# A gated delta-net layer with a table-coded FFN: substitution steps moved within the slots, FFN weight pieces gathered in one slot

## The chip, the cores and the metric

The kernel runs on one core of a Trainium2 chip. The metric is the device time of one execution in microseconds (us). Three executions of the kernel before took 4345.69, 4349.83 and 4350.42 us; the median is 4349.83 us.

## The reference

The input is `x` of 4 x 1024 x 256 in f32. Two residual blocks are applied, each with a layer norm before and after it. The first is a gated delta net with 16 key heads and 32 value heads of 128, worked in chunks of 64 tokens:

```
mixed = silu(conv4(x @ W_qkv))             # causal convolution over 4 tokens
q, k = l2n(q), l2n(k)
A  = -(k_beta @ k.T * decay) * strict      # per chunk and head, 64 x 64
Tm = solve_triangular(eye - A, eye)        # unit lower triangular inverse
u, kcd = Tm @ v_beta, Tm @ (k_beta * exp(gc))
# scan over the chunks, with a state St of 128 x 128 per head
v_new = u - kcd @ St
out   = (q * exp(g)) @ St + (q @ k.T * decay) @ v_new
St    = St * exp(g_last) + (k * exp(g_last - g)).T @ v_new
y = (rmsnorm(out) * norm_w * silu(x @ W_z)) @ W_out
```

The second block is an FFN, `silu(gate) * up`, whose three weight matrices are given as indices into a table of 16 values (`w = lut[idx]`).

## The kernel before, in words

The work is cut into 8 groups of 4 value heads. In a group there are 32 units: one chunk of 64 tokens of two batch rows together, so that 128 rows are filled. 8 units make a "super"; there are 32 supers. The compute engines' order is written out by hand: each engine runs its instructions in exactly the order in which the program issues them, and so does SyncE's DMA queue, and each instruction waits by semaphore for what it needs.

The main loop (line 1024 on) goes over **slots**, one for each unit of the scan, with a lead of 21 slots for preparation. A slot is written as a string of names in `SLOTS`, picked by `iq`, the slot's place in its super, so the pattern repeats every 8 slots; "slot 5" below is the slot with iq 5. What the names issue:

- `A` and `B`: one `channel` each, a projection of 128 channels (`pp`, 8 matmuls, L423) and its convolution: one tap on ScalarE (`cv`, L437), then three on VectorE (L440) that are put off by a place or two, then silu on ScalarE (L444).
- `N0`, `N1`, `N2`: the newer unit's `step`: transposes of v (`pv`) and their scaling to `x0`; the state's products (`pkqs`, L684) with four VectorE operations that add them to `x0` (L695) and `qs` on ScalarE; then the inverse times `x0` (`px`, L704), `yg` from it on VectorE (L712), and the state's decay on GpSimd (`S`, L721).
- `O3`, `J`, `O4`: the older unit's end: `po` and `core` (L728), the sums of squares on ScalarE (`junk`, L733), then `pu` (L741) and the state's update on VectorE (`S`, L748).
- `Z`, `T`, `U`: the gated output: `pz` (L143) and silu `zs` (L782) at `Z`; two GpSimd products `zs` (L784, L786), issued one and two places behind it; `pto` and `oT`; `pout` (L797) and the sum `ac` on VectorE (L802).
- `n`, `s`, `r`, `q`: norms, scores and rms. Scores end in `kkq` with `lT` and `aT` on VectorE (L556) in slots 2, 3, 6 and 7; in between, GpSimd forms the decay matrix `dc`: four operations (L530, L531) issued at the end of slots 0 and 4, and two (L537) at the end of slots 1 and 5, after exponentials on ScalarE (L534).
- `v1`: one call of `invert`, the **forward substitution**: 32 matrices of 32 x 32 in each of four partition groups are inverted column by column. The first call loads `lb` and sets `v`; each of the 31 others is one step j with two VectorE operations, an outer product `rank` (L580) and its subtraction from `v` (L581), both of (j+1)(31-j) elements per partition (31 to 256), and both with two operands in SBUF. A number behind the `v` is the number of calls.
- `b`: `build`, in slots 3 and 4. It begins with a ScalarE copy of `v` (`lb`, L593) and sends `v` through DRAM into the padded matrices of the matmuls `m` (L612, L626).

A super's inversion begins in slot 4 and is spread over slots 4 to 7, 0, 1 and 2; what is left of it at the end of slot 2 is drained there (`if inv and iq == 2`). After `O4` each slot also issues one **piece** of the FFN's weights (`next(pieces, None)`): one GpSimd comparison with a table entry (L301, TENSOR_SCALAR) and one addition (L305, TENSOR_TENSOR). There are 224 pieces.

PSUM gives the main loop four single banks and two double ones (`two_banks`). The double ones are used in turn by A's `pp`, `pu` and B's `pp`, so a slot's `pu` writes the bank that the preceding slot's B filled, and must wait for that B's last `cv` tap.

Of the kernel before, what the change touches and what calls it, by code (L numbers as in the profile page):

```python
# [15 lines left out]
B, S, HID = 4, 1024, 256  # L16
# [48 lines left out]
def delta_net_ffn_kernel(  # L65
# [18 lines left out]
    V, A, G_, T_ = nc.vector, nc.scalar, nc.gpsimd, nc.tensor  # L84
# [84 lines left out]
    def layer_norm_stats(pool, src, n, tag):  # L169

        mv = pool.tile([P, n, 2], F32, tag=f"mv{tag}", name=f"mv{tag}")
        for i in range(n):
            st = pool.tile([P, 6], F32, tag=f"st{tag}", name=f"st{tag}")
            V.bn_stats(st, src(i))
            V.bn_aggr(mv[:, i, :], st)
        r = pool.tile([P, n], F32, tag=f"r{tag}", name=f"r{tag}")
        G_.tensor_scalar_add(r, mv[:, :, 1], LN_EPS)
        G_.tensor_tensor(r, r, bc(rsqrt, [P, n]), ALU.pow)
        return mv, r
# [14 lines left out]
    with tc.tile_pool(name="pre", bufs=2) as pre, tc.tile_pool(name="gates", bufs=1) as gp:  # L194
# [13 lines left out]
        for s in range(NSB):  # L208
# [4 lines left out]
            mv, r = layer_norm_stats(pre, lambda i: xt[:, i, :], SB, "a")  # L213
# [70 lines left out]
    def lut_pieces(pool):  # L284

        jobs = []
        for n, idx in ((0, gidx), (1, uidx)):
            for r in range(KC):
                for h in range(INTER // PIECE):
                    rows, cols = slice(r * P, (r + 1) * P), slice(h * PIECE, (h + 1) * PIECE)  # L290
                    jobs.append((idx[rows, cols], wgu_d[n, rows, cols], P, PIECE))
        for r, n in I_TILES:
            jobs.append((didx[r : r + n, :], wd_d[r : r + n, :], n, HID))
        for src, dst, n, cols in jobs:
            ix = pool.tile([P, PIECE], I32, tag="lx", name="lx")
            w = pool.tile([P, PIECE], F32, tag="lw", name="lw")
            nc.sync.dma_start(ix[:n, :cols], src)
            for e in range(NLUT):
                t = pool.tile([P, PIECE], F32, tag="lt", name="lt") if e else None
                o = t if e else w  # L300
                G_.tensor_scalar(  # L301
                    o[:n, :cols], ix[:n, :cols], float(e), lutb[:n, e : e + 1], ALU.is_equal, ALU.mult
                )
                if e:
                    G_.tensor_add(w[:n, :cols], w[:n, :cols], t[:n, :cols])  # L305
                yield
            nc.sync.dma_start(dst, w[:n, :cols])

    with ExitStack() as main:
# [4 lines left out]
        pieces = lut_pieces(sc)  # L314
# [500 lines left out]
        def resume(gen):  # L815
            nonlocal count
            wait = next(gen, None)
            if wait:
                heappush(due, (place + wait, count, gen))
                count += 1  # L820

        def go(gen):

            nonlocal place
            late = [entry for entry in due if entry[2] is gen]
            while late:
                due.remove(late[0])
                heapify(due)
                resume(gen)
                late = [entry for entry in due if entry[2] is gen]  # L830
            if gen is not None:
                resume(gen)
            place += 1
            while due and due[0][0] <= place:
                resume(heappop(due)[2])
# [7 lines left out]
        def work(kind, n, *args):  # L843

            if not 0 <= n < len(supers):
                return None
            key = (kind, n, *args)
            if key not in started:
                started[key] = kind(supers[n], *args)
            return started[key]  # L850
# [3 lines left out]

        LQ = 2 * SB + 5
        LV = SB // 2
        SLOTS = [
            "A v1 O3 s N0 v1 T n J O4 v1 N1 Z v1 B n N2 U n s",  # L860
            "A v1 O3 N0 v1 T J v1 O4 N1 r Z v1 B N2 q s U",
            "A v1 O3 N0 v1 T J v1 O4 v1 N1 Z s v1 B N2 n U",
            "b A O3 N0 T J O4 N1 Z s B N2 U b",
            "v1 A b O3 s N0 v1 T n J O4 v1 N1 Z v1 B n N2 v1 U n s",
            "A v1 O3 N0 v1 T J v1 O4 v1 N1 r Z v1 B N2 q s v1 U",
            "A v1 O3 N0 v1 T J v1 O4 v1 N1 Z s v1 B N2 n v1 U",
            "A v1 O3 N0 v1 T J v1 O4 v1 N1 Z s v1 B N2 v1 U",
        ]


# [152 lines left out]
        with tc.manual_schedule(engines=COMPUTE):  # L1023
            for s in range(-LQ, len(units)):
                n, i = divmod(s, SB)
                nq, iq = divmod(s + LQ, SB)
                nv, iv = divmod(s + LV, SB)
                gens = {}
                newer = step(*units[s]) if s >= 0 else None
                for c in "01234":  # L1030
                    gens["N" + c], gens["O" + c] = newer, older
                gens["J"] = older
                gens["T"] = gens["U"] = gated
                gated = project_out(*units[s - OUT_LAG]) if s >= OUT_LAG else None
                gens["Z"] = gated
                if 0 <= nv < len(supers):
                    gens["A"] = channel(supers[nv], iv // 4, 2 * MG + iv % 4, 2)
                if nq < len(supers):
                    gens["B"] = channel(supers[nq], iq // 4, iq % 4, 1)
                inv = work(invert, nq - 1 if iq >= 4 else nq - 2)  # L1040
                made = work(build, nq - 2)

                root = [work(rms, *divmod(s // 4 - 1, 2))] + ([work(roots, n + 1)] if i == 4 else [])

                ahead = units[s + 1] if 0 <= s + 1 < len(units) else None
                if ahead and ahead[1]:
                    expand(*ahead)
                for name in SLOTS[iq].split():
                    c = name[0]
                    if c == "v":  # L1050
                        for _ in range(int(name[1:]) if inv else 0):
                            next(inv, None)
                        continue
                    block = 2 * nq + iq // 4 - (iq % 4 != 2 or c == "s")
                    if c in "rq":
                        for gen in filter(None, root[: 1 if c == "r" else 2]):
                            resume(gen)
                        continue
                    if c == "n":
                        gen = work(norms, *divmod(block, 2))  # L1060
                    elif c == "s":
                        gen = work(scores, *divmod(block, 2))
                    elif c == "b":
                        gen = made
                    else:
                        gen = gens.get(name)
                    go(gen)
                    if name == "O4":
                        next(pieces, None)
                        if ahead and not ahead[1]:  # L1070
                            expand(*ahead)
                if inv and iq == 2:
                    drain(inv)
                older = newer
                if s >= EARLY:
                    next(early, None)
            drain(older)
            drain(rms(supers[-1], 1))
            drain(*(gen for _, _, gen in sorted(due)))
            drain(early)  # L1080
            last_ffn()
            rest = [gated] + [project_out(*unit) for unit in units[len(units) - OUT_LAG :]]
            part = gate_up(0)
            while rest or part:
                for gen in rest[:2]:
                    if next(gen, END) is END:
                        rest.remove(gen)
                if part and next(part, END) is END:
                    part = None
            for v in range(NU):  # L1090
                nxt = gate_up(v + 1) if v + 1 < NU else None

                side = [ended(v - 1, range(4))] if v else []
                if 4 <= v + 2 < NU:
                    side.append(prepared(v + 2))
                    next(side[-1])
                side = chain(*side)
                if nxt:
                    next(nxt)
                for i in range(4):  # L1100
                    down(v, i)
                    next(side, None)
                    if not nxt:
                        drain(ended(v, [i]))
                while nxt and next(nxt, END) is not END:
                    next(side, None)
                drain(side)
# [51 lines left out]
```

## Time and profile before

| | |
|---|---|
| median of 3 runs | 4349.83 us |
| the profiled execution: its own time, its span | 4347.06 us, 4345.3 us |
| granted TensorE clock, mean | 0.98 |
| busy: TensorE, VectorE, ScalarE, GpSimd | 92%, 81%, 61%, 48% of the span |
| `rank` (L580) and `v` (L581), 992 operations each | 467.2 and 553.3 us on VectorE |
| pieces (L301 and L305), all forms | some 470 us on GpSimd, the last one at 3269.7 us |
| first and last `rank` | 172.4 and 3906.3 us |

Reading: PE is TensorE's matmuls, DVE is VectorE, ACT ScalarE, POOL GpSimd, SP SyncE. A row of a group gives the line, the engine, the operation, what it writes and reads, the shape and the count; behind the bar are the busy time, the mean of one in ns, and the engine's idle time just before. A row of the timeline gives start, duration, engine, line, operation and, in brackets, how long the engine sat idle before and for whom. A row of windows gives a stretch, its length, and for each engine its busy time and number of instructions in it.

The main loop's steady part is a chain of 32 supers of about 121 us each. The slots of one of them begin with A's `pp` at 1781.7 (slot 4), 1797.6 (5), 1813.6 (6), 1830.3 (7), 1845.8 (0), 1860.4 (1), 1873.4 (2) and 1888.0 us (3); the next super begins at 1902.9 us.

### The profile page before, as it was taken

The numbers are of one execution on the slowest core, as the hardware profiler recorded it, in microseconds if no ns is written. First come the engines' busy times: TensorE is split into PE (matmuls) and PEld (weight loads), VectorE is DVE, ScalarE is ACT, GpSimd is POOL, SyncE is SP. The second block draws the span as 40 slices with busy tenths as digits, with TensorE's granted clock in tenths as the row PEclk, the third lists the DMA queues.
The fourth block names the chain that finished last, engine by engine and source line by source line (L and its number), as shares of the span: only waits on it lengthen the run. The fifth ranks groups of instructions, "written<-read, shape, count | busy, mean of one in ns | idle before, by whom it ended". The sixth has DMA issues, their size and how long they took to land.

```text
span 4345.3 us, 79442 instructions
## 1 busy us (share of the span) xinstructions
PE 3992.3 (92%) x26664; PEld 2858.5 (66%) x26664; DVE 3517.0 (81%) x6641; ACT 2646.9 (61%) x6573; POOL 2082.5 (48%) x1782
## 2 busy tenths in 40 slices
PE   3679999999999999999999999999999999999999
PEld 3456667677666666676766667676766776666454
DVE  4788888888888888888888988888888898886243
ACT  2456667666666666666666666666666666656211
POOL 2545564655555554655455554555554343434122
PEclk7899999999999999999999999999999999999999
DMA  3444444444444454444454444544445444443011
GB/s 88 124 107 113 111 112 124 121 130 119 126 130 118 107 133 125 134 117 119 125 135 128 109 114 128 133 118 114 132 128 128 115 120 121 130 108 96 26 39 29
DMA packets 1053124, 492.72 MB, mean 113 GB/s; under 512 B 730528, under 2 KB 951856, under 8 KB 1052720
## 3 DMA queue, kind: packets, MB, share of 16 engines
q1 hardware_dynamic: 1052720, 487.64, 42.5%
q8 instruction: 216, 3.54, 0.3%
q14 instruction: 188, 1.54, 0.1%
HBM read 267.66 MB, written 219.69 MB: 112 GB/s over the span
## 4 chain that ended last, share of the span: by engine, by line
PE 57%; DVE 25%; issue 7%; ACT 6%; POOL 3%; DMA 1%; SPq 1%; DVEq 0%; POOLq 0%; ACTq 0%
PE pp L423 13%; DVE cv L440 9%; PE pout L797 7%; PE pz L143 7%; PE pkqs L684 6%; DVE rank L580 4%; PE pgu L960 4%; PE px L704 4%; PE pu L741 3%; PE po L704 3%; DVE v L581 2%; PE kkq L546 2%; PE py L976 2%; DVE core L728 2%; PE pto L790 1%
## 5 line engine op out<-in xcount | busy, mean ns | idle before, releaser
L440 DVE SCALAR_TENSOR_TENSOR cv<-pp,cw,cv 128x512 f32<-128x512 f32 x1536 | 1148.9, 748 | 352.2 <-ACT cv L437 322.7
L784 POOL TENSOR_TENSOR zs<-zs,rr 128x512 f32<-128x512 f32 x256 | 267.0, 1043 | 1558.3 <-ACT zs L782 1549.3
L437 ACT ACTIVATE cv<-pp,cw 128x512 f32<-128x512 f32 x512 | 350.9, 685 | 486.0 <-PE pp L423 486.0
L581 DVE TENSOR_TENSOR v<-v,rank 128x31 f32<-128x31 f32 (+15 forms) x992 | 553.3, 558 | 34.1
L423 PE MATMUL pp<-xnT,wq 128*128 128x262 f32 x2048 | 531.0, 401 | 43.3 <-DVE cv L440 34.6
L423 PEld LDWEIGHTS pp<-xnT,wq 128*128 128x128 f32 x2048 | 371.7, 191 | 216.6 <-issue 58.7
L423 PE MATMUL pp<-xnT,wv 128*128 128x262 f32 x2048 | 503.0, 387 | 5.8 <-DVE cv L440 5.8
L797 PE MATMUL pout<-wo,oT 128*128 128x256 f32 x2048 | 504.9, 391 | 0.7 <-ACT oT L792 0.7
L143 PE MATMUL pz<-wzs,xnT 128*64 128x512 f32 x2048 | 487.1, 596 | 4.7 <-DVE ac L802 3.8
L580 DVE TENSOR_TENSOR rank<-v,lb 128x31 f32<-128x31 f32 (+15 forms) x992 | 467.2, 471 | 25.9 <-DMA lb<-ltd 20.1
L684 PE MATMUL pkqs<-S,qku 128*64 128x256 f32 x3840 | 478.1, 387 | 5.2 <-DVE core L728 3.5
L721 POOL TENSOR_TENSOR S<-S,dkm 128x1024 f32<-128x1024 f32 x224 | 436.7, 1949 | 26.5 <-PE pkqs L684 16.1
L704 PE MATMUL px<-x,ue 128*128 128x128 f32 x2048 | 292.9, 287 | 168.2 <-issue 108.1
L704 PEld LDWEIGHTS px<-x,ue 128*128 128x128 f32 x2048 | 264.1, 194 | 269.0 <-issue 151.1
L423 PEld LDWEIGHTS pp<-xnT,wv 128*128 128x128 f32 x2048 | 381.5, 190 | 73.8 <-issue 13.1
L797 PEld LDWEIGHTS pout<-wo,oT 128*128 128x128 f32 x2048 | 384.1, 198 | 49.4 <-issue 3.4
L684 PEld LDWEIGHTS pkqs<-S,qku 128*64 128x64 f32 x3840 | 248.7, 136 | 204.2 <-issue 49.2
L733 ACT ACTIVATE junk<-core 128x128 f32<-128x128 f32 x1024 | 318.5, 311 | 82.4 <-DVE core L728 53.9
L786 POOL TENSOR_TENSOR zs<-zs,core 128x512 f32<-128x512 f32 x256 | 328.6, 1284 | 20.0
L709 ACT ACTIVATE xs<-px 128x512 f32<-128x512 f32 x256 | 154.8, 605 | 236.2 <-PE px L704 236.2
L444 ACT ACTIVATE qk<-cv 128x512 f32<-128x512 f32 x256 | 161.2, 630 | 206.1 <-DVE cv L440 202.6
L741 PE MATMUL pu<-yg,kt 64*128 64x256 f32 x1920 | 272.2, 402 | 14.5 <-DVE cv L440 13.1
(187 smaller groups left out, 7198.4 us busy)
## 6 DMA issues: line engine op xcount, KB each, us to landing
qkd<-qk SPq DMA_DIRECT2D x256, 256.0 KB, 2.6
qku<-qkd SPq DMA_DIRECT2D x256, 256.0 KB, 2.9
dc<-rows_d SPq DMA_DIRECT2D x256, 128.0 KB, 3.4
ltd<-lT SPq DMA_DIRECT2D x128, 256.0 KB, 2.5
atd<-aT SPq DMA_DIRECT2D x128, 256.0 KB, 2.8
ae<-atd SPq DMA_DIRECT2D x512, 64.0 KB, 2.6
acc_d<-ac SPq DMA_DIRECT2D x256, 128.0 KB, 2.2
ac<-acc_d SPq DMA_DIRECT2D x224, 128.0 KB, 2.6
```

The lines of the kernel that those rows point to most:

```text
L143: T_.matmul(ps[ab * C : (ab + 1) * C, :], lhsT=xnT[:, kc, 2 * p + ab, H + n * C : H + (n + 1) * C], rhs=rhs(kc), start=kc == 0, stop=kc == ...
L423: T_.matmul(ps[:, 2 * p : 2 * p + 2, : H + BT], lhsT=wt[:, kc, :], rhs=xnT[:, kc, 2 * p : 2 * p + 2, c0 : c0 + H + BT], start=kc == 0, sto ...
L437: A.activation(cv, ps[:, :, H : H + BT], AF.Copy, scale=cw[:, ch, H : H + 1])
L440: V.scalar_tensor_tensor(cv, ps[:, :, i : i + BT], cw[:, ch, i : i + 1], cv, ALU.mult, ALU.add)
L580: V.tensor_tensor(t, bc(v[:, 0 : j + 1, j : j + 1], sh), bc(lb[:, j : j + 1, j + 1 :], sh), ALU.mult)
L581: V.tensor_tensor(v[:, 0 : j + 1, j + 1 :], v[:, 0 : j + 1, j + 1 :], t, ALU.subtract)
L684: T_.matmul(as4(ps)[ab * C : (ab + 1) * C, two, :], lhsT=qk[:, m, j, ab, :], rhs=S_[:, ab, two, :], start=True, stop=True,)
L704: T_.matmul(as4(ps)[:, h, :], lhsT=w[:, h, :], rhs=src[:, h, :], start=True, stop=True)
L721: G_.tensor_tensor(flat, flat, bc(decay, [P, 2 * HG, P]), ALU.mult)
L741: T_.matmul(as4(pu[:, ab])[:, two, :], lhsT=kt[half, m, :], rhs=yg[half, two, :], start=True, stop=True)
L786: G_.tensor_tensor(zs, zs, k.cores.pop(u), ALU.mult)
L797: T_.matmul(pp[:, :HID], lhsT=oT[:, h, :], rhs=wo[:, h, :], start=h == 0, stop=h == HG - 1)
```

## The change

The calls of `invert` are put at other places of the slot strings, and their number per slot changes; the pieces are issued by a table, 0, 1 or 3 to a slot.

```diff
+        PIECES = 1, 0, 1, 3, 1, 0, 1, 0
         SLOTS = [
-            "A v1 O3 s N0 v1 T n J O4 v1 N1 Z v1 B n N2 U n s",
-            "A v1 O3 N0 v1 T J v1 O4 N1 r Z v1 B N2 q s U",
-            "A v1 O3 N0 v1 T J v1 O4 v1 N1 Z s v1 B N2 n U",
+            "A v1 O3 s v1 N0 v1 T n J O4 N1 v2 Z B n N2 U n s",
+            "A O3 N0 T J O4 N1 v2 r Z B N2 q s U",
+            "A v1 O3 v1 N0 v2 T J O4 N1 v2 Z s B N2 n U",
             "b A O3 N0 T J O4 N1 Z s B N2 U b",
-            "v1 A b O3 s N0 v1 T n J O4 v1 N1 Z v1 B n N2 v1 U n s",
-            "A v1 O3 N0 v1 T J v1 O4 v1 N1 r Z v1 B N2 q s v1 U",
-            "A v1 O3 N0 v1 T J v1 O4 v1 N1 Z s v1 B N2 n v1 U",
-            "A v1 O3 N0 v1 T J v1 O4 v1 N1 Z s v1 B N2 v1 U",
+            "v1 A b O3 s v1 N0 v1 T n J O4 N1 v2 Z B n N2 U n s",
+            "A O3 N0 T J O4 N1 v2 r Z B N2 q s U",
+            "A v1 O3 v1 N0 v1 T J O4 N1 v2 Z s B N2 n U",
+            "A v1 O3 v1 N0 v2 T J O4 N1 v2 Z s B N2 U",
         ]
...
                     if name == "O4":
-                        next(pieces, None)
+                        for _ in range(PIECES[iq]):
+                            next(pieces, None)
```

The steps j that fall into each slot, in the order in which a super's inversion runs:

| slot | 4 | 5 | 6 | 7 | 0 | 1 | 2 | 3 |
|---|---|---|---|---|---|---|---|---|
| before | load, 0-3 | 4-9 | 10-15 | 16-21 | 22-25 | 26-29 | 30 | none |
| changed | load, 0-3 | 4-5 | 6-10 | 11-16 | 17-21 | 22-23 | 24-29, and 30 at the slot's end | none |
| pieces, changed | 1 | 0 | 1 | 0 | 1 | 0 | 1 | 3 |

No step stands behind `Z` or between `T` and `N1` any more; in slots 4, 6, 7, 0 and 2 steps stand in the first part of the slot too, and in each slot with steps two stand between `N1` and `Z`.

## The prediction

> **What bounds the kernel now.** I read the page first (chain, groups), then the windows of the eight slots of one super, then the timeline of the worst slot, engine by engine.
>
> ```profile
> PE 57%; DVE 25%; issue 7%; ACT 6%; POOL 3%; DMA 1%; SPq 1%; DVEq 0%; POOLq 0%; ACTq 0%
> ```
>
> TensorE holds most of the chain, VectorE a quarter. The windows tell in which slots (length, then busy time and count of PE, PEld, DVE, ACT, POOL):
>
> ```profile
> 1781.70:1797.60 15.90, 15.90 (x130) 11.04 (x127) 9.85 (x21) 11.17 (x28) 7.98 (x8) 1.00 0.52 120
> 1797.60:1813.60 16.00, 13.37 (x84) 9.68 (x83) 15.44 (x30) 8.14 (x22) 11.31 (x10) 1.00 0.41 94
> 1813.60:1830.30 16.70, 14.38 (x100) 10.55 (x100) 16.32 (x29) 12.79 (x30) 10.71 (x9) 1.00 0.28 67
> 1830.30:1845.80 15.50, 14.07 (x99) 10.60 (x98) 15.15 (x29) 7.87 (x23) 6.40 (x5) 1.00 0.60 179
> 1845.80:1860.40 14.60, 14.60 (x95) 10.18 (x94) 12.86 (x28) 9.03 (x25) 2.73 (x3) 1.00 0.45 125
> 1860.40:1873.40 13.00, 13.00 (x84) 9.80 (x83) 12.58 (x24) 8.88 (x23) 11.66 (x10) 1.00 0.29 75
> 1873.40:1888.00 14.60, 14.37 (x100) 10.57 (x100) 13.43 (x25) 13.13 (x32) 7.60 (x8) 1.00 0.48 131
> 1888.00:1902.90 14.90, 14.90 (x131) 11.29 (x129) 10.58 (x19) 9.66 (x24) 8.05 (x9) 1.00 0.71 196
> ```
>
> These are slots 4, 5, 6, 7, 0, 1, 2, 3. In 4, 0, 1 and 3 PE is never idle. In 5, 6 and 7, with six steps each, it idles 2.63, 2.32 and 1.43 us and VectorE hardly at all: there VectorE bounds. The timeline of slot 6 shows why (the last two rows are GpSimd's and PE's):
>
> ```profile
> 1823.54 1.23 DVE L748 TENSOR_TENSOR S<-pu,S 128x1024 f32<-128x1024 f32 x1
> 1824.68 0.82 DVE L580 TENSOR_TENSOR rank<-v,lb 128x252 f32<-128x252 f32 x1
> 1825.54 1.37 DVE L581 TENSOR_TENSOR v<-v,rank 128x252 f32<-128x252 f32 x1
> 1826.83 1.11 DVE L695 SCALAR_TENSOR_TENSOR x<-pkqs,dkm,x 128x128 f32<-128x128 f32 x4
> ...
> 1825.31 1.32 POOL L786 TENSOR_TENSOR zs<-zs,core 128x512 f32<-128x512 f32 x1
> ...
> 1827.37 1.13 PE L704 MATMUL px<-x,ue 128*128 128x128 f32 x8 [2.07 <-issue]
> ```
>
> One step stands ahead of `x`; its `rank` ends 0.27 us behind the `zs` product L784 (1824.19 to 1825.23), its `v` 0.28 us behind L786 (1826.63). PE waits 2.07 us. The same operations alone take little more than one ns an element; by size:
>
> ```profile
> L581 DVE TENSOR_TENSOR v<-v,rank 128x135 f32<-128x135 f32 x64 | 68.5, 1070 | 2.2
> L581 DVE TENSOR_TENSOR v<-v,rank 128x156 f32<-128x156 f32 x64 | 20.8, 325 | 2.2
> ```
>
> Fewer elements take three times as long: the place in the slot decides, not the size. 156 elements at 325 ns and 256 at 425 give 0.17 us + 1.0 ns an element; the 31 steps have 5456 elements, so 2 x (31 x 0.17 + 5456 x 0.001) = 21.5 us a super, against (467.2 + 553.3)/32 = 31.9 measured. So **10.4 us a super are waits on GpSimd's TENSOR_TENSORs**, one for one.
>
> **What the change does, part by part.** A super costs 120.4 us ((3906.3 - 172.4)/31, from the `rank` rows). I scale by 30, for 32 supers of which some at group ends are shorter.
>
> *Pieces.* In the super from 3343.4 us no piece runs any more (GpSimd's L301 busy 0.00), and it takes 121.6 us, against 121.2 with eight pieces. So moving them is worth 0, at most 0.4 x 30 = 12 us either way. Three in slot 3 (2.4 us each by the rows, 1.44 + 0.92) delay nobody there: the next GpSimd work, `zs` at 1897.4, comes 9.4 us behind the slot's start. No wait, load or queue is added: each piece's DMAs move with it past at most three slots, and the last piece is done about slot 257 of 277 instead of 225, 4 slots ahead of `begin_ffn`.
>
> The Trainium skill, "SBUF — State Buffer", § Who interferes with whom, says that a VectorE instruction with two SBUF inputs contends with any GpSimd instruction that reads SBUF, and that the second to issue blocks fully. The rows agree for TENSOR_TENSOR, but not for the pieces' TENSOR_SCALAR: during L301 (1828.76, 1.44 us) `v` on 255 elements took 0.42 us. By the page each L301 met by a step would cost up to 1.44 us; for the three slots freed of theirs that would make the sum 3 x 1.44 x 30 = 130 us lower.
>
> *Slot 5, two steps instead of six.* Both come behind `x`. Slot 1 has the same tiles and takes 13.0 us with PE always busy: 16.0 to about 13.2, **-2.7** (no more, since the mean super is 0.8 us shorter than this one).
>
> *Slot 6, five instead of six, three of them ahead of `x`.* Slot 2 has the same tiles, so I start from its rows: ScalarE, behind the exponentials, ends its `cv` at 6.29 us into the slot and VectorE's first tap starts at 6.33. Behind it now come tap 0.75, step 7 0.8 (+0.5 behind the piece's L305), two taps 1.55, step 8 0.85, `S` 1.2, `x` 1.1: done at 13.1; PE starts `px` about 0.55 us ahead of that (as at 1827.37, with `x` ending 1827.94), and 2.9 us later the slot ends (1827.37 to 1830.3): 15.4 instead of 16.7. **-1.2.**
>
> *Then the two steps between `N1` and `Z`: the new place is not ahead of the `zs` products.* L784 starts 2.56 us behind the last tap (1882.09 to 1884.65 in slot 2: silu of `vt`, four `qs`, silu of `zs` on ScalarE). VectorE needs `S` + `x` = 2.3 us plus its steps from there. In slots 6, 7 and 2, with steps behind the taps, the pair thus starts when `zs` does. In slot 6: taps done at 10.0, L784 12.5 to 13.55, L786 to 14.85, `S` decay (1.95) to 16.85. From 13.1 the four operations wait for one each: 13.8, 15.1, 17.1, 17.5; alone they would end at 14.8. Queued behind them are `lT`, `aT`, B's taps, `yg`: 1.3 + 0.75 + 0.7 + 1.5 = 4.25, until 21.7, **6.3 us into slot 7** (now 2.46). `pu` needs that bank and starts 3.6 us into an unhindered slot: 2.7 late.
>
> *Slot 7.* From 6.3: `ac` 0.35, step 0.9, `core` 0.65, tap 0.75, step 0.9, two taps 1.55, two steps 1.85, `S` 1.2, `x` 1.1 = 15.55; minus 0.55 plus 2.9 = 17.9, against 15.5 here; I take **+1.5**, since slot 7 varies with slot 6. Its pair waits for L786 and the decay (to about 18.2), ends at 19.35, the tail at 23.6, 5.7 into slot 0.
>
> *Slot 0.* `pu` 2.1 late; now PE is never idle there: **+1.6**. Norms keep `zs` later in this slot, so its pair is free and VectorE catches up. *Slot 1:* pair, `eq` and `rr` against the same three GpSimd products, as `eq` and `rr` alone today: 0.
>
> *Slot 2, seven steps instead of one.* Four ahead of `x` add 2.6 less today's wait of 1.4 (step 30): `px` 0.7 to 2.6 late, **+1.2**. *Slot 3:* the second pair collides as in slot 6, the tail reaches 5.7 into slot 3, `pu` 2.1 late; and step 30, now last in slot 2, ends near 6.4, so `lb` on ScalarE (2.0 us) starts there, not at 1.59, with A's `cv` queued behind it: **+2.2**, nothing less than 0.2. SP holds `vd` for step 30 with later loads behind it, used a slot later. Slot 3's four idle microseconds (14.9 - 10.58 on DVE) of VectorE then absorb the rest.
>
> **Sum:** -2.7 - 1.2 + 1.5 + 1.6 + 0 + 1.2 + 2.2 = **+2.6 us a super**, x 30 = +78. The profiled execution has 4347; 4425, and 3 more for the median: **4428 us**.
>
> **Rivals.** *Faster: the waits go.* If ScalarE's silu comes later than I have it, or VectorE gets ahead, the pair slips in before `zs` in every slot. Then slot 5 gives -2.7, 6 and 7 -2.0 and -1.0, and slot 3 costs 0.3 to 1.5: -5.4 to -4.2 a super, 4188 to 4224. For it: slot 4's and slot 3's gaps behind `x` (0.6 us and more). Against: the 2.56 us above hold `zs` and `x` together. In between, with slots 7 and 0 at half of my price and slots 2 and 3 at +1.5, the super is -0.9, 4323. Chance of faster, both: 0.28.
>
> *Level:* gains of slots 5 and 6 just pay for the rest: 4341 to 4359, 0.06.
>
> *Slower, and worse:* slots 7 and 0 at full price (+2.4, +2.1) and slot 2 at +2.6: +5.4 a super, 4510. Of the 0.66 for slower, my sum has 0.45 and this 0.21.
>
> **The numbers.** Likeliest's own range 4370 to 4490. For 8 in 10 I leave out the better half of the faster case (0.12) and the end of the worse (0.07): 4240 to 4500. About 0.2% can be told from no change in this measurement: faster 0.28, within 0.06, slower 0.66.
>
> **What would show it.** Right: PE idle gone in slot 5, about as long idle in 7, new in 0, 2 and 3, ahead of `pu` by `cv` L440; mean of `v` and `rank` hardly below 558 and 471 ns; `lb` L593 waiting for `v`. Wrong: `v` and `rank` near 350 ns, and PE never idle in slots 6 and 7; then the pair stands ahead of `zs`, and my coupling of `zs` to the last tap is the step that fails.

## The result, and the profile after

The changed kernel takes **4444.01 us** (median of 4 runs, 4442.11 to 4445.07) against 4347.76 of the kernel before on the same chip: a ratio of 1.0222, 95% interval 1.0204 to 1.0239. The forecast was 4428, range 4240 to 4500. The profiled execution's span is 4442.0 us, 96.7 more than before.

The page's chain has moved from TensorE to VectorE, ScalarE and DMA:

```profile
PE 47%; DVE 31%; ACT 9%; DMA 5%; issue 5%; SPq 2%; POOL 1%; DVEq 0%; ACTq 0%; POOLq 0%
```

The windows of the changed kernel, for one super from slot 4 to slot 3 (columns as in the prediction):

```profile
1839.50:1855.50 16.00, 16.00 (x131) 11.10 (x128) 9.92 (x22) 11.16 (x28) 10.90 (x11) 1.00 0.66 159
1855.50:1868.50 13.00, 13.00 (x85) 9.77 (x84) 10.93 (x24) 8.17 (x22) 8.42 (x8) 1.00 0.47 114
1868.50:1882.80 14.30, 14.10 (x100) 10.52 (x99) 11.51 (x21) 12.77 (x30) 7.85 (x8) 1.00 0.46 111
1882.80:1900.60 17.80, 15.80 (x100) 11.44 (x99) 17.45 (x29) 7.87 (x23) 6.12 (x5) 0.90 0.39 117
1900.60:1916.80 16.20, 14.88 (x95) 10.16 (x94) 15.78 (x30) 9.01 (x25) 3.54 (x3) 1.00 0.50 133
1916.80:1929.80 13.00, 13.00 (x84) 9.79 (x83) 12.58 (x23) 8.74 (x23) 10.27 (x9) 1.00 0.30 78
1929.80:1945.20 15.40, 14.34 (x99) 10.53 (x99) 14.99 (x27) 13.18 (x32) 8.42 (x8) 1.00 0.27 71
1945.20:1963.50 18.30, 15.62 (x132) 11.27 (x130) 15.36 (x27) 9.68 (x24) 12.52 (x11) 1.00 0.63 165
```

Slot 5 (second row) no longer idles on PE and takes 13.0 us instead of 16.0, slot 6 14.3 instead of 16.7. Slots 7, 0, 2 and 3 are longer, and there PE now idles 2.0, 1.3, 1.1 and 2.7 us while VectorE is busy nearly throughout in slots 7, 0 and 2. Mean slot lengths, over 24 supers of each trace (from one start of A's `pp` to the next):

| slot | 4 | 5 | 6 | 7 | 0 | 1 | 2 | 3 | super |
|---|---|---|---|---|---|---|---|---|---|
| before | 15.62 | 15.13 | 16.00 | 16.32 | 14.62 | 13.00 | 14.38 | 14.92 | 120.0 |
| changed | 16.01 | 12.32 | 14.14 | 16.47 | 17.03 | 13.00 | 15.18 | 18.85 | 123.0 |
| forecast difference | 0 | -2.7 | -1.2 | +1.5 | +1.6 | 0 | +1.2 | +2.2 | +2.6 |
| measured difference | +0.4 | -2.8 | -1.9 | +0.2 | +2.4 | 0 | +0.8 | +3.9 | +3.0 |

3.0 us on 32 supers are the 96.7. Two things lie behind these means. Slot 7 takes 15.5 us before in three supers of four, and 17.6 to 19.7 in every fourth; in the changed kernel it takes mostly 16.8, and 14.6 to 14.7 in every fourth. And in slot 7 of the super shown the granted clock is at 0.50 for 3.4 us (0.90 over the slot): the five slots 7 of the changed kernel with such a stretch take 17.8 to 18.0 us.

The pair between `N1` and `Z` of slot 6, in the timeline of the changed kernel, VectorE first, then GpSimd:

```profile
1879.32 1.11 DVE L695 SCALAR_TENSOR_TENSOR x<-pkqs,dkm,x 128x128 f32<-128x128 f32 x4
1880.36 0.77 DVE L580 TENSOR_TENSOR rank<-v,lb 128x220 f32<-128x220 f32 x1
1881.16 1.34 DVE L581 TENSOR_TENSOR v<-v,rank 128x220 f32<-128x220 f32 x1
1882.53 1.98 DVE L580 TENSOR_TENSOR rank<-v,lb 128x231 f32<-128x231 f32 x1
1884.54 0.40 DVE L581 TENSOR_TENSOR v<-v,rank 128x231 f32<-128x231 f32 x1
...
1879.84 1.04 POOL L784 TENSOR_TENSOR zs<-zs,rr 128x512 f32<-128x512 f32 x1 [3.92 <-ACT zs L782]
1880.95 1.30 POOL L786 TENSOR_TENSOR zs<-zs,core 128x512 f32<-128x512 f32 x1
1882.21 2.04 POOL L721 TENSOR_TENSOR S<-S,dkm 128x1024 f32<-128x1024 f32 x1
```

Each of the first three ends 0.25 us behind one GpSimd product: 1881.13 behind 1880.88, 1882.50 behind 1882.25, 1884.51 behind 1884.25; the fourth, free, takes 0.40. What stands behind them is late for TensorE in slot 7:

```profile
1886.20 0.66 PE L671 MATMUL pv<-ident,vt 128*128 128x128 f32 x4 [0.59 <-DVE aT L556]
1887.54 0.63 PE L790 MATMUL pto<-ident,zs 128*128 128x128 f32 x4 [0.69 <-DVE yg L712]
1888.89 2.08 PE L741 MATMUL pu<-yg,kt 64*128 64x256 f32 x8 [0.72 <-DVE cv L440]
```

`pu` starts 6.1 us into the slot; the prediction had 6.3. `pv` and `pto` wait too, for PSUM banks that `aT` and `yg` still read. Over the whole run, PE's idle time ahead of `pu` (behind the second bar; before, then changed):

```profile
L741 PE MATMUL pu<-yg,kt 64*128 64x256 f32 x1920 | 272.2, 402 | 14.5 <-DVE cv L440 13.1
L741 PE MATMUL pu<-yg,kt 64*128 64x256 f32 x1920 | 279.7, 411 | 64.5 <-DVE cv L440 64.5
```

Ahead of `pz` it grows from 4.7 to 33.4 us, 33.0 of them for `x0` from ScalarE.

### The profile page after: what moved, and what is told of

The parts are those of the page before. It is cut to its first block, busy times and chain, and to the rows that moved or that the text cites. A ratio compares the mean times of both kernels' runs of the same rounds, so it can differ in the third digit from the quotient of the medians.

```text
span 4442.0 us, 79504 instructions
## 1 busy us (share of the span) xinstructions
PE 4022.4 (91%) x26664; PEld 2854.2 (64%) x26664; DVE 3602.9 (81%) x6641; ACT 2643.1 (60%) x6573; POOL 2078.5 (47%) x1782
## 4 chain that ended last, share of the span: by engine, by line
PE 47%; DVE 31%; ACT 9%; DMA 5%; issue 5%; SPq 2%; POOL 1%; DVEq 0%; ACTq 0%; POOLq 0%
PE pp L423 10%; DVE cv L440 8%; DVE rank L580 6%; PE pz L143 6%; PE pkqs L684 5%; DVE v L581 5%; PE pout L797 4%; PE pgu L962 4%; PE px L704 3%; PE pu L741 3%; PE po L704 2%; DVE S L748 2%; DVE x L695 2%; PE py L978 2%; PE pn L474 1%
## 5 line engine op out<-in xcount | busy, mean ns | idle before, releaser
L580 DVE TENSOR_TENSOR rank<-v,lb 128x31 f32<-128x31 f32 (+15 forms) x992 | 508.5, 513 | 60.8 <-DMA lb<-ltd 45.2
L143 PE MATMUL pz<-wzs,xnT 128*64 128x512 f32 x2048 | 487.2, 596 | 33.4 <-ACT x L675 33.0
L797 PE MATMUL pout<-wo,oT 128*128 128x256 f32 x2048 | 486.6, 381 | 0.7 <-ACT oT L792 0.7
L423 PEld LDWEIGHTS pp<-xnT,wv 128*128 128x128 f32 x2048 | 384.6, 192 | 76.4 <-issue 14.1
L797 PEld LDWEIGHTS pout<-wo,oT 128*128 128x128 f32 x2048 | 370.7, 191 | 44.6 <-issue 3.4
L143 PEld LDWEIGHTS pz<-wzs,xnT 128*64 128x64 f32 x2048 | 141.3, 137 | 230.4 <-issue 150.0
```

The source lines that it names most:

```text
L143: T_.matmul(ps[ab * C : (ab + 1) * C, :], lhsT=xnT[:, kc, 2 * p + ab, H + n * C : H + (n + 1) * C], rhs=rhs(kc), start=kc == 0, stop=kc == ...
L423: T_.matmul(ps[:, 2 * p : 2 * p + 2, : H + BT], lhsT=wt[:, kc, :], rhs=xnT[:, kc, 2 * p : 2 * p + 2, c0 : c0 + H + BT], start=kc == 0, sto ...
L580: V.tensor_tensor(t, bc(v[:, 0 : j + 1, j : j + 1], sh), bc(lb[:, j : j + 1, j + 1 :], sh), ALU.mult)
L797: T_.matmul(pp[:, :HID], lhsT=oT[:, h, :], rhs=wo[:, h, :], start=h == 0, stop=h == HG - 1)
```

## The experiments

All ratios are against the kernel before, on the same chip. My theory: the steps' new places cost the time, by waits on GpSimd's products, and by the late end of `v` in slot 3. Rivals: the pieces; the order on VectorE without any waits.

**e1, the pieces alone; e2, the steps alone.**

```diff
# e1: before with PIECES = 1, 0, 1, 3, 1, 0, 1, 0
# e2: changed with
-        PIECES = 1, 0, 1, 3, 1, 0, 1, 0
+        PIECES = 1, 1, 1, 1, 1, 1, 1, 1
```

> The slot strings of before, the pieces by the new table (1, 0, 1, 3, 1, 0, 1, 0). Theory (the time comes from the steps alone): 4348 us, within 0.3% of before. Rival (three pieces in slot 3 hold GpSimd for 7 us and cost something there): over 4375 us, with PE idle in slot 3.

> The slot strings of the changed kernel, one piece in each slot as before. Theory (steps alone): 4444 us, within 0.3% of the changed kernel. Rival (pieces have a part in it): under 4415 us.

e1 took 4348.39 us, ratio 1.0003 (0.9994 to 1.0012). e2 took 4422.37, ratio 1.0178 (1.0163 to 1.0193). The pieces alone cost nothing in the total, but behind the changed steps the table costs 22 us: neither text fits whole. e2's trace differs in slots 3 (18.13 us) and 4 (15.62): `m` waits less for `pad` (15.5 us in all, against 31.2 in the changed kernel, 6.4 before and 13.4 in e1). The changed kernel's timeline of a slot 3 that begins at 1574.75 and takes 22 us shows why, GpSimd first, then SyncE's queue:

```profile
1580.79 1.48 POOL L301 TENSOR_SCALAR lt<-lx,lutb 128x344 f32<-128x344 int32 x1
1582.35 0.92 POOL L305 TENSOR_TENSOR lw<-lw,lt 128x344 f32<-128x344 f32 x1
...
1577.63 1.11 SPq L523 DMA_DIRECT2D dc<-rows_d  x2
1583.29 0.33 SPq L307 DMA_DIRECT2D wgu_d<-lw  x1
1583.66 0.43 SPq L297 DMA_DIRECT2D lx<-in_uidx  x1
1584.20 0.38 SPq L446 DMA_DIRECT2D qkd<-qk  x1
...
1588.89 0.82 SPq L607 DMA_DIRECT2D pad<-vd  x2
```

The slot's third piece is the last of its 16; its store (L307) stands in the queue ahead of `vd` and the pads' loads and waits for the addition, until 1583.27. Nothing is issued from 1578.74 to 1583.29, though `qk` is done at 1580.55 and `v` at 1580.98; their stores go out at 1584.20 and 1585.39. The pads begin 14.1 us into this slot; in the same slot of e2 they begin at 9.9. What is said of SyncE's queue ahead of the prediction does not hold: its order is not the program's. The program issues this store with the next piece, in slot 4, and `vd` at the end of slot 2. SyncE is not among the engines whose order is written out, and the rows show the store ahead of `vd`.

Six of the 14 stores fall into a slot 3 of the changed kernel. These six slots take 19.5 to 22.1 us, the others 18.4 in the mean; with the slots 4 behind them they are 26 us longer than the others, which is about what the table costs. e1 is not free of it: four of its slots 3 with a store take 15.8 to 17.7 us instead of 15.0, but its slots 2, 6 and 7 are about 0.2 us a super shorter.

**e11, the pieces in the slots with steps.**

```diff
-        PIECES = 1, 0, 1, 3, 1, 0, 1, 0
+        PIECES = 2, 0, 2, 0, 2, 0, 2, 0
```

> The changed strings with two pieces in slots 0, 2, 4 and 6 and none in slot 3. Theory (the table's 22 us come from SyncE: the store of a finished piece stands in its queue ahead of the pads' loads and waits until GpSimd has done slot 3's three pieces): 4415 to 4430 us, like one piece a slot. Rival (they come from the pieces' additions, which hold steps): over 4444 us, since more of them now meet steps.

4419.84 us, ratio 1.0167 (1.0150 to 1.0184). With none in slot 3 the 22 us are gone, though steps wait longer behind additions (1.3 us a super against 1.0): the queue, not the additions.

**e3, slot 5's new string alone; e10, and slot 2's last step ahead of `x`.**

```diff
# e3, in before
-            "A v1 O3 N0 v1 T J v1 O4 v1 N1 r Z v1 B N2 q s v1 U",
+            "A O3 N0 T J O4 N1 v2 r Z B N2 q s U",
# e10, besides
-            "A v1 O3 N0 v1 T J v1 O4 v1 N1 Z s v1 B N2 n U",
+            "A v1 O3 N0 v1 T J v2 O4 v1 N1 Z s B N2 n U",
```

> Before, with the changed string in slot 5 alone: two steps there, both behind N1, and the four others done later, so that slot 2 does five small steps (26 to 30) by its own unchanged calls. Theory: slot 5 keeps its -2.7 us a super, slot 2 gives back 0.7 to 1.5; 4290 to 4312 us. Rival (VectorE has the same work and the gain of slot 5 is only handed on to slots 6, 7 and 2): 4338 to 4358 us.

> The kernel before with the changed string in slot 5, and in slot 2 the last of its five calls moved from behind Z to between J and O4, so that all its steps stand ahead of x. Theory (a step behind Z waits for the zs products and makes v and B's taps late for slot 3): slot 3 falls from 16.0 to about 15.0 us, slot 2 rises by 0.3; 4307 - 0.7 x 32 = 4284 us. Rival (the step costs as much ahead of x): 4300 to 4312 us.

e3 took 4306.70 us, ratio 0.9908 (0.9892 to 0.9925): the time as expected, and faster than both kernels. Slot 5 takes 12.30 us. What is paid for it is not paid in slot 2, as expected (14.4, unchanged), but in slots 3 (16.02), 7 and 1 (0.5 and 0.4 us), while slot 6 gains 1.0. The change thus has one part that gains. e10 took 4317.24, ratio 0.9931 (0.9917 to 0.9946), a miss: slot 3 does return to 14.92, but slot 2 rises from 14.41 to 15.73 instead of by 0.3. A step ahead of `x` in slot 2 costs more than one behind `Z`, and more than the rival had allowed (4312).

**e4, step 30 in the pair.**

```diff
-            "A v1 O3 v1 N0 v2 T J O4 N1 v2 Z s B N2 n U",
+            "A v1 O3 v1 N0 v2 T J v1 O4 N1 v2 Z s B N2 n U",
```

> The changed kernel with one more call in slot 2 between J and O4, so that step 30 is in the pair behind N1 and nothing is left for the slot's end. Theory: lb on ScalarE starts about 1.5 us into slot 3 instead of 6.1, the wait of pz for x0 and of m for pad goes (some 2.2 us a super), less 0.4 for the longer way to x in slot 2: 4444 - 1.8 x 30 = 4390 us. Rival (slot 3 pays for the late taps alone, and ScalarE would have been late anyway): 4435 to 4450 us.

4408.69 us, ratio 1.0140 (1.0125 to 1.0156): 35 us less than the changed kernel, of 54 expected. Slot 3 falls from 18.85 to 17.26, but `lb` starts at 5.4 us into the slot (median), not at 1.5. The changed kernel's ScalarE shows what else holds it (slot 3 begins at 1945.2):

```profile
1950.57 0.63 ACT L444 ACTIVATE qk<-cv 128x512 f32<-128x512 f32 x1 [5.20 <-DVE cv L440]
1951.32 2.00 ACT L593 COPY lb<-v 128x1024 f32<-128x1024 f32 x1
1953.23 0.68 ACT L437 ACTIVATE cv<-pp,cw 128x512 f32<-128x512 f32 x1
```

Ahead of `lb` in ScalarE's order stands the silu of slot 2's B, and that waits for B's taps, late behind the pair. Step 30 holds `lb` only for the last 0.1 to 0.5 us; the late taps hold it for the rest. Slot 3 falls by more than `lb` gains, since with step 30 `v`'s own store (L584) is early too: it goes out 0.9 us into the slot instead of 6.9, and the last load of the pads at 14.3 instead of 17.0 (medians).

**e5 and e6, both kernels without the three products.**

```diff
-            G_.tensor_tensor(zs, zs, bc(k.rr[u // 4][:, u % 4, :].unsqueeze(2), h4), ALU.mult)
             yield 1
-            G_.tensor_tensor(zs, zs, k.cores.pop(u), ALU.mult)
+            k.cores.pop(u)
...
-                    G_.tensor_tensor(flat, flat, bc(decay, [P, 2 * HG, P]), ALU.mult)
```

> The changed kernel without GpSimd's two zs products (L784, L786: the rms scale and the gated output are left out, pto reads silu of z) and without the state's decay (L721); the other GpSimd work stays. Theory (the pair behind N1 is late because each of its operations waits for one of these three): the waits of rank and v fall from 33.4 - 21.5 = 11.9 us a super to under 3, no more idle PE in slots 7, 0 and 3 ahead of pu; 4090 to 4190 us, and within 50 us of the kernel before with the same left out. Rival (the order on VectorE itself is worse, with seven steps in slot 2 and the last one late): it stays 90 us or more above that kernel.

> The kernel before with the same left out (the two zs products and the state's decay). Theory: some 180 of the 330 us that its steps wait go, and so does most of the idle PE of slots 5 to 7: 4110 to 4210 us. Rival (steps wait, but PE would be held by something else): over 4280 us.

e5 took 4240.40 us, ratio 0.9761 (0.9733 to 0.9789), 50 us over its range; e6 4190.84, ratio 0.9647 (0.9619 to 0.9675), as expected. The distance of the two falls from 96 to 50 us. So the three products account for about half of the loss. 50 us stay when they are gone, the most that my theory allowed and less than the 90 of the rival: slots 0 and 2, where more steps stand, and slot 3 behind them are 1.1 to 1.3 us longer than in e6, slots 6 and 7 0.5 and 1.6 us shorter. These 50 us are not the order alone. e5 keeps the table of pieces, and its slots 3 that a store delays, with the slots 4 behind them, are some 12 us longer than its others. Its steps also still wait more than e6's. By what `v` and `rank` take beyond 0.17 us + 1.0 ns an element, the waits are 12.2 us a super in the changed kernel and 5.0 in e5 (under 3 expected), most of these behind `dc`, which now runs earlier; 10.9 before and 2.7 in e6.

**e7 and e8, the state's decay by scalars, in before and in the changed kernel.**

```diff
-                    decay = el[:, ti].rearrange("p a h -> p (a h)").unsqueeze(2)
-                    G_.tensor_tensor(flat, flat, bc(decay, [P, 2 * HG, P]), ALU.mult)
+                    decay = el[:, ti].rearrange("p a h -> p (a h)")
+                    for i in range(2 * HG):
+                        G_.tensor_scalar_mul(flat[:, i, :], flat[:, i, :], decay[:, i : i + 1])
```

> The kernel before with the state's decay as eight TENSOR_SCALAR operations of 128 elements on GpSimd, one for each matrix, instead of one TENSOR_TENSOR of 1024. Theory (a step waits for a TENSOR_TENSOR, not for a TENSOR_SCALAR): rank and v lose the 1.4 us waits behind L721, some 50 us in all; 4290 to 4340 us if GpSimd's eight take under 5 us together. Rival (any GpSimd operation that reads SBUF holds the step): no faster than 4340 us, and steps that wait for one of the eight after the other.

> The changed kernel with the same decay by scalars. Its steps wait about 140 us in all for L721. Theory: these go, 4.3 us of VectorE's time a super, and over half of it is on the path: 4340 to 4390 us. Rival: 4435 us or more.

e8 took 4325.23 us, ratio 0.9945 (0.9930 to 0.9961): 119 less than the changed kernel, more than expected, and less than before. Its timeline of the same pair in slot 6, VectorE and then GpSimd:

```profile
1829.92 0.77 DVE L580 TENSOR_TENSOR rank<-v,lb 128x220 f32<-128x220 f32 x1
1830.72 1.34 DVE L581 TENSOR_TENSOR v<-v,rank 128x220 f32<-128x220 f32 x1
1832.10 0.45 DVE L580 TENSOR_TENSOR rank<-v,lb 128x231 f32<-128x231 f32 x1
1832.58 0.55 DVE L581 TENSOR_TENSOR v<-v,rank 128x231 f32<-128x231 f32 x1
...
1830.52 1.29 POOL L787 TENSOR_TENSOR zs<-zs,core 128x512 f32<-128x512 f32 x1
1831.80 4.79 POOL L722 TENSOR_SCALAR S<-S,dkm 128x128 f32<-128x128 f32 x8
```

The first two operations are as in the changed kernel to the hundredth; the third takes 0.45 us instead of 1.98, under a decay that is 2.5 times as long. The Trainium skill, "SBUF — State Buffer", § Who interferes with whom, has a two-input VectorE instruction contend with any GpSimd instruction that reads SBUF; these rows differ for TENSOR_SCALAR.

e7 took 4349.56 us, ratio 1.0010 (0.9999 to 1.0022): a miss. The waits behind the decay went (1.45 to about 0.1 us a super), but at 0.62 us a piece the eight take 5 us, and `dc` comes later. Step 30 in slot 2 no longer meets it (1.0 us before), but the steps in slot 1 meet it for 2.0 us a super instead of 1.0 and those in slot 6 for 1.3 instead of 1.1 (in all 4.9, before 4.7). What slot 5 gains (15.13 to 14.07), slots 6 (16.00 to 16.93) and 1 (13.00 to 13.63) pay; why slot 6 pays more than its steps wait is not shown. In e8 slots 5 and 1 keep 12.30 and 13.00 us, with two steps each, both late. With the decay by scalars in both, the changed order is thus the faster one by 24 us, where it was the slower one by 96.

**e9, what helped, together; e12, a third step in slots 5 and 1.**

```diff
# e9: changed, with e8's decay, e4's slot 2, one piece a slot
# e12: e9 with
-            "A O3 N0 T J O4 N1 v2 r Z B N2 q s U",               # slots 1 and 5
+            "A O3 N0 T J v1 O4 N1 v2 r Z B N2 q s U",
-            "A v1 O3 v1 N0 v2 T J v1 O4 N1 v2 Z s B N2 n U",     # slot 2
+            "A v1 O3 v1 N0 v1 T J O4 N1 v2 Z s B N2 n U",
```

> Three parts together on the changed strings: the decay by eight TENSOR_SCALARs, step 30 in slot 2's pair behind N1, one piece in every slot. If the parts found so far add up, a super loses the 2.8 us that slot 3 still idles with the decay by scalars, and 0.6 in slot 4, and pays 0.4 in slot 2: 4325 - 2.6 x 32 = 4240 us, below both kernels. If slot 3's idle time has another cause than the late end of v and the pads behind it: 4290 us or more.

> The version e9 (decay by scalars, one piece a slot) with a third step in slots 5 and 1, between J and O4, and so two fewer in slot 2 (five, all but the pair ahead of N0's taps). Theory (slots 5 and 1 have room ahead of x, since PE is never idle in them; slot 2's seven are what makes it 16.1 us and v late): slot 2 falls by about 1.2 us, slot 3 by 0.4, slots 5 and 1 stay within 0.2; 4274 - 1.4 x 32 = 4229 us. Rival (the third step meets the decay matrix's operations, which the longer decay now pushes into slots 5 and 1, and is paid there): 4265 us or more.

e9 took **4274.38 us**, ratio 0.9833 (0.9818 to 0.9848), the fastest of those that leave nothing out, though 34 us above the 4240 of its expectation (whose terms make 3.0 us a super, not 2.6). Slot 4 gives the 0.6 us expected (15.61), slot 3 2.2 of the 2.8 (15.65), and slot 2 with seven steps costs 1.4 instead of 0.4. e12 took 4288.57, ratio 0.9865 (0.9849 to 0.9882), a miss: slot 2 falls to 15.26, slots 5 and 1 stay at 12.30 and 13.00, but `v` and `rank` take 33.6 us a super instead of 29.2, and slots 6 (14.6 instead of 13.9) and 3 (16.3 instead of 15.7) pay. Of the 4.4 us some 2.4 are waits behind the `zs` products, which the pair now meets since it starts later, and 2.3 behind `dc`. The time is the rival's, and so is half of its cause, but it is not slots 5 and 1 that pay.

## Why the prediction was right, step by step

- *Slot 5, -2.7:* right, -2.8; e3 shows that it is real and not handed on whole.
- *Slot 6, -1.2:* -1.9. ScalarE's `cv` ended 5.6 us into the slot, not at slot 2's 6.29: slot 6 has no `roots` on ScalarE ahead of it. The pair's collision was as worked out, one for one.
- *Slots 7 and 0, +1.5 and +1.6:* +0.2 and +2.4, together +2.6 against +3.1. The mechanism (tail late, `pu` late) is in the rows. The split was off because slot 7 is not one case: from 15.5 to 16.8 us in most supers, +1.3 and near the forecast, but some 4 us shorter in every fourth, where it took 17.6 to 19.7 before. The prediction read one super. Slot 0's pair, called free, waits 0.8 us behind the first `zs` product.
- *Slot 2, +1.2:* +0.8.
- *Slot 3, +2.2:* +3.9, the term most mis-sized. Two things were missing. The first is the pads behind a piece's store in SyncE's queue (the steps "moving them is worth 0" and "No wait, load or queue is added": alone the table is worth 0, but with `v` and `lb` late the pads have no slack left, and it is 22 us; e1, e2, e11). That is 0.7 us of slot 3 and all of slot 4's +0.4, which the prediction did not have. The second is that `lb` stands behind the silu of late taps (e4).
- *The waits, one for one, and `zs` tied to the last tap:* right; means of `v` and `rank` 564 and 513 ns, not below before's. But they are not all: of the 96 us, 50 stay in e5 and e6. Some 12 of these are the stores', and e5's steps still wait 2.3 us a super longer than e6's; what is left for the order itself, and how much of it is slot 2's count and how much slot 0's, was not tried apart.
- *The sum, +2.6:* +3.0. That it came so near is partly luck: slots 5, 6, 7 and 2 came out 2.5 us lower than forecast, slots 0, 3 and 4 2.9 us higher.

## What to carry to other kernels

Where two engines block each other, a place in the program order is not a place in time: work out when the engine that lags really gets there, from the rows that tie the other engine's start to it. A move that is free alone can cost once another part of the same change has used up the slack behind it, and an in-order DMA queue is where to look: a store that waits for a slow producer holds each load behind it.

## What the runs showed of the hardware

- A VectorE operation with two SBUF inputs waited in full for a GpSimd TENSOR_TENSOR (up to 1.6 us behind 1024 elements), and hardly for a TENSOR_SCALAR, on int32 (1.44 us long, `v` of 255 elements in 0.42) or f32 with a scalar per partition (above).
- Eight GpSimd TENSOR_SCALARs of 128 elements took 0.61 to 0.62 us each in the mean, 5 us together; the one TENSOR_TENSOR of 1024 took 1.95.
- One DMA that waited for its data in SyncE's queue held the DMAs behind it, whose data were ready: nothing went out from 1578.74 to 1583.29 us.
- The granted clock fell to 0.50 for 3.4 us at a time, a dozen times in the changed kernel's main loop. It did so in slot 7 of the super shown (0.90 over the slot), and not in slot 3, where TensorE idled longer (1.00); what sets it is not shown.
